# Two list parts scattered under the attention, and counts read into registers as steps of the plan

## The chip, the cores and the metric

The kernel runs on one core of one Trainium2 chip. The metric is device time in microseconds (us); the times before are the median of three runs. The engines are named as the profile names them: PE (TensorE; PEld is its weight load), DVE (VectorE), ACT (ScalarE), POOL (GpSimd) and SP (SyncE, which issues DMAs).

## What is computed

The reference is one transformer block with adaptive layer norms, on 2 x 2048 tokens of 256 features in float32: a causal attention with two query heads that share keys and values, and then a mixture of eight experts (hidden width 1024) in which a token goes to each expert whose gate exceeds a threshold of its own. Cut to what matters:

```python
h = _layernorm(x) * (1 + ca) + sa
x = x + ga * attention(h)                       # 2 heads of 128, causal
h = _layernorm(x) * (1 + cb) + sb
gate = softmax(h @ Wg + bg)                     # 8 experts
thr = sigmoid(h @ Wt + bt) * 0.125              # one threshold for each token
w = (gate - thr) * (gate - thr >= 0)
w = w / sum(w)                                  # where the sum is not 0
y = gelu(einsum('td,edf->etf', h, W1) + b1)
out = einsum('te,etd->td', w, einsum('etf,efd->etd', y, W2) + b2)
x = x + gb * out
```

How many tokens an expert gets is known only when the gates have been computed. The kernel computes each expert on its own tokens alone.

## The kernel before

**Attention, as a plan.** The first part (`attention`) treats 32 tiles of 128 tokens. Each piece of work is a step given to a small planner (`Plan`): its engine, an estimated cost, the steps that it comes after, and a rank. The planner plays the steps through with these costs, lets an engine that is free take the ready step of lowest rank, and the instructions of each engine are then issued in that fixed order. `late` is a time after the end of a step before its followers count as ready. Tiles go in groups of four (the last ones of two and one), alternating between the two batches; the tile number is the rank.

For each tile, POOL computes the two inverse deviations of the layer norms (`rstda`, `rstdf`, L418 and L419) and splits the normed features into halves (`hp`, L677) for storing in `feats`. PE turns the normed tile `hx` (`ph`, L692) for the gates.

**Lists.** Each expert has a list in HBM, of token number and weights. `place` holds where an entry goes in the list of each expert, `entry` what is written. A column of `place` belongs to one tile. List 0 is filled under the attention: after each group, `gate_steps` computes the places (L804) and adds one POOL step for each tile (`scatter`, L807), an indirect DMA of 128 entries, ranked ten behind the group. The first 512 tokens of expert 0 (`AHEAD` items) are worked on at the end of the attention, where that many are there. The last steps compute the counts (`total`, L849 to L868): the tokens of each expert, the number of its whole items less one, capped at eight (`more`), and eight less that.

**Experts, as programs.** The second part (`experts`) is five programs, one for each engine, that loop over items of 256 tokens and wait for one another by semaphores. The number of rounds is read at run time from the tile `counts` into registers (`count`, which calls `values_load`, L1035); PE, ACT and DVE read all the counts of the experts at the beginning of their programs. DVE increments `ready` for the first time only after its nine reads, and PE waits for it before its first matmul.

For an item, POOL copies its indices (`at`, L1296), gathers its 256 rows from `feats` (`xr`, L1254), SP transposes them (`xp`, L1100), DVE joins the halves to `xT` (L1196), PE multiplies with the first weights (`h`, L1142) and the second ones (`y`, L1133), with ACT's gelu between (`g`, L1168), DVE forms the weighted result `yo` (L1232), and POOL adds it to the output with two indirect DMAs (`out`, L1285). `xT`, `xp`, `xr` and `yo` exist once. The weights of expert e + 2 are loaded by ACT when it begins expert e (L1177, L1180). An expert's last item may be a half one, of 128 tokens.

The lists of experts 1 to 7 are written here, each during the expert before, in eight parts of four columns (`write`, L1267 to L1275: two copies and four indirect DMAs). POOL hands out a part in each of an expert's first items; parts for which there are too few items go ahead of them (`front`). Expert 0's program writes the first part of list 1 once more at its very start, before the counts are read:

```python
write(1, 0, 0)
skip = count(pool, 3 * E, AHEAD * CI)
```

SP reads a list into its sheet (`read`, L1090) once all its parts have landed. Between the two parts of the kernel all engines meet (L1075, L1418).

Of the kernel before, what the change touches and what calls it, by code (L numbers as in the profile page):

```python
# [18 lines left out]
ALU = mybir.AluOpType  # L19
# [13 lines left out]
NW = 4  # L33
NP = NTOK // P // NW
AHEAD = 2
AHEAD_TILES = 24
SC = 512
EPS = 1e-5
# [63 lines left out]
def adaln_block_kernel(ctx, tc, x, wqkvT, woT, wgt, bgt, w1, b1T, w2, b2, cT, wmod, rope, out):  # L102
# [49 lines left out]
        yo=[const.tile([P, CI, D], F32, name=f"yo_{k}") for k in range(AHEAD)],  # L152
        who=const.tile([P, CI], I32, name="who"),
        xT=const.tile([P, KD, TI], F32, name="xT"),
    )

    with tc.manual_schedule():
# [35 lines left out]
def attention(  # L193
# [522 lines left out]
    def gate_steps(b, i0, m, q, group, after):  # L716
# [86 lines left out]
            nc.vector.tensor_scalar(col, col, 7, None, ALU.logical_shift_right)  # L803
            nc.vector.tensor_tensor(dst, dst, col, ALU.add)  # L804

        def scatter(j):
            nc.gpsimd.indirect_dma_start(  # L807
                out=lists[0],
                out_offset=bass.IndirectOffsetOnAxis(ap=place[:, at + j, 0:1], axis=0),
                in_=entry[:, at + j, 0, :],  # L810
                in_offset=None,
            )

# [105 lines left out]
    for k in range(AHEAD):  # L919
# [71 lines left out]
        for c in range(CI):  # L991
            for f0 in (0, NF // 2):
# [4 lines left out]
                    give=["s"] * (NF // 2) if (c, f0) == (CI - 1, NF // 2) else [],  # L997
                )
        low("DVE", 1.5, result, [n, n_g, l_b2], give=["ps", "size"])

    n_s = low(
        "SP", 0.1, lambda: nc.sync.dma_start(kept.sheet, sheet_of_0), listed, late=2.0
# [10 lines left out]
            next_at, next_at, flag[:, 0:1], number[:, :CI], ALU.mult, ALU.add  # L1013
        )

    n = low("DVE", 0.4, behind, [n_s, n_flag])
    fetch(lambda c: next_at[:, c : c + 1], "_next", [n], lambda: kept.xT)

    plan.add("PE", 0.2, total, after=[last, n_flag], take=["ps"], give=["ps"], rank=q)
    plan.run()  # L1020
    ctx.close()


def experts(
# [5 lines left out]

    LAG = 2
    xT, who, yo = kept.xT, kept.who, kept.yo[-1]

    def count(eng, at, most):
        return nc.values_load(  # L1035
            counts[0:1, at : at + 1], engines=[eng.engine],
            skip_runtime_bounds_check_because="from a sum of 0s and 1s over all tokens",
            min_val=0, max_val=most,
        )

    def run(eng, many, most, do):
        with eng.If(many > 0):
# [32 lines left out]
    with tc.tile_critical():  # L1075
# [7 lines left out]
        with nc.Block() as block:  # L1083

            @block.sync
            def _(sync):
                def read(e):

                    sync.wait_ge(sem["written"], (e * NP + 1) * (16 * NW))
                    sync.dma_start(  # L1090
                        sheets[e], lists[e].rearrange("(p c) f -> p c f", p=P)
                    ).then_inc(sem["read"], 16)

                def turn(t):

                    sync.wait_ge(sem["loaded"], t * (16 * CI))
                    sync.sem_inc(sem["paused"], 1)
                    sync.wait_ge(sem["ready"], t + 1)
                    sync.sem_inc(sem["paused"], 1)
                    sync.dma_start_transpose(xp, xr).then_inc(sem["planed"], 16)  # L1100

                sync.sem_inc(sem["planed"], 16)
                done, t0 = 1, 0
                for e in range(E):
                    many = items_of(sync, count(sync, e, NTOK))
                    if e == E - 1:
                        run(sync, many, NTOK // TI, lambda i: turn(t0 + i))
                    else:
                        a = count(sync, E + e, NP)
# [12 lines left out]

            @block.tensor
            def _(pe):
# [29 lines left out]
                        pe.wait_ge(here[e], 32)  # L1154

                pe.sem_inc(sem["taken"], 1)
                n = [count(pe, e, NTOK) for e in range(E)]
                items(pe, n, item, begin)

            @block.scalar  # L1160
            def _(act):
# [20 lines left out]
                        ).then_inc(here[e + RES], 16)  # L1182

                act.sem_inc(sem["second"], 4)
                items(act, [count(act, e, NTOK) for e in range(E)], item, begin)

            @block.vector
            def _(dve):
# [48 lines left out]
                    if e > 0:  # L1237
                        dve.wait_ge(sem["read"], 16 * e)

                n = [count(dve, e, NTOK) for e in range(E)]  # L1240
                skip = count(dve, 3 * E, AHEAD * CI)
                dve.sem_inc(sem["ready"], 2)
                items(dve, n, item, begin)

# [1 line left out]
            def _(pool):  # L1246
# [11 lines left out]
                            in_offset=bass.IndirectOffsetOnAxis(ap=at[:, c : c + 1], axis=0),  # L1258
                        ).then_inc(sem["loaded"], 16)

                def write(e, c, w=None):

                    if w is None:
                        w = c + (e - 1) * NP
                        wait("written", w * (16 * NW) + 16 * NW)
                        w = w + 1
                    pool.tensor_copy(  # L1267
                        to, place[:, ds(c * NW, NW), e : e + 1].rearrange("p c o -> p (c o)")
                    ).then_inc(sem["staged"], 1)
# [55 lines left out]
                            compute_op=ALU.add,  # L1325
                        ).then_inc(sem["added"], 16)
                pool.sem_inc(sem["biased"], AHEAD)
                write(1, 0, 0)
                skip = count(pool, 3 * E, AHEAD * CI)
                done, t0 = 1, 0  # L1330
                for e in range(E):
                    many = items_of(pool, count(pool, e, NTOK))
                    if e > 0:
                        wait("read", 16 * e)
                    if e == E - 1:
                        run(pool, many, NTOK // TI, lambda i: item(e, i, t0 + i))
                    else:
                        a, front = count(pool, E + e, NP), count(pool, 2 * E + e, NP)

                        def part(c):  # L1340
                            write(e + 1, nc.s_assert_within(c, 0, NP - 1,
                                skip_runtime_bounds_check_because="a part of a list"))
# [20 lines left out]
                add(t0)  # L1363

                single = pool.snap(
                    ((count(pool, E - 1, NTOK) + (P - 1)) >> 7) & 1, min_val=0, max_val=1
                )
                with pool.If(single > 0):
                    add(t0 + 1, 1)
# [52 lines left out]
```

## Time and profile before

| | us |
|---|---|
| median of three runs (lowest to highest) | 1696.54 (1695.61 to 1699.3) |
| the profiled execution | 1694.8 |
| its span in the profile | 1693.0 |
| attention and the work ahead, until PE's first h of L1142 | 526.1 |
| experts' programs, from there to the end | 1166.9 |

In the profile a row of the timeline has the start, the duration (both in us), the engine, the line of the kernel, the operation, and what it writes and reads; in brackets stands how long the engine was idle before it and what released it. A row of the waits has the engine and line that waited, what it waited for, the sum in us, how often, and the longest. A row of the chain has start, duration and what. A row of the windows has the stretch, its length, the busy time of PE, PEld, DVE, ACT and POOL with the number of instructions, the granted PE clock, the DMA share and GB/s. A name with q (PEldq) is an engine's sequencer: there the three durations are the least, the median and the most, in ns.

### The profile page before, as it was taken

How to read it: one execution, taken by the hardware profiler on the slowest of the kernel's cores; microseconds unless marked ns; L12 is line 12 of the kernel's file. 1: busy time of each engine (PE TensorE's matmuls, PEld its weight loads, DVE VectorE, ACT ScalarE, POOL GpSimd, SP SyncE). 2: the span in 40 equal slices, each digit the busy share in tenths (PEclk: the TensorE clock that was granted, in tenths of full speed). 3: DMA queues.
4: the chain of work that ended last, by engine and by line, in shares of the span. 5: the costliest groups of instructions: out<-in, count | busy, mean ns of one | idle time of the engine just before them, and what ended most of it. 6: DMA issues, size and time to landing. Idle time of an engine off the chain costs nothing.

```text
span 1693.0 us, 26695 instructions
## 1 busy us (share of the span) xinstructions
PE 1627.9 (96%) x7666; PEld 1354.3 (80%) x7666; DVE 677.9 (40%) x2220; ACT 575.1 (34%) x1390; POOL 855.9 (51%) x991
## 2 busy tenths in 40 slices
PE   6898999999998997999999999999999999999997
PEld 3666666677777886888888888888888888888886
DVE  5886666566652322223332222223222232222322
ACT  1544555555551222222222222222322232222222
POOL 2332322111125777765776775676677467744443
PEclk9999999999999998999999999999999999999998
DMA  6310100000013335333434533433533343333333
GB/s 210 102 36 26 38 20 29 22 11 19 14 40 92 59 62 109 56 63 62 103 61 64 109 59 66 106 61 59 106 59 59 65 63 57 64 56 59 65 56 47
DMA packets 166046, 106.36 MB, mean 63 GB/s; under 512 B 111137, under 2 KB 157345, under 8 KB 165857
## 3 DMA queue, kind: packets, MB, share of 16 engines
q0 software_dynamic: 42064, 46.84, 17.3%
q1 hardware_dynamic: 116048, 46.22, 11.8%
q10 hardware_dynamic: 7872, 12.58, 2.3%
q8 instruction: 26, 0.43, 0.1%
q14 instruction: 36, 0.29, 0.1%
HBM read 50.39 MB, written 31.87 MB: 49 GB/s over the span
## 4 chain that ended last, share of the span: by engine, by line
PE 60%; DMA 3%; POOL 2%; issue 2%; POOLq 0%; DVE 0%; SPq 0%; DVEq 0%
PE h L1142 30%; PE y L1133 30%; DMA xp<-xr 2%; POOL out L1285 1%; DMA xr<-feats,at 1%; POOL list L1275 0%; DMA out<-yo,who 0%; POOL xr L1254 0%; POOLq L1035 0%; POOL out L1317 0%; POOL at L1296 0%; POOLq L1083 0%; POOLq L1296 0%; DVE yo L1232 0%; DVE xT L896 0%
## 5 line engine op out<-in xcount | busy, mean ns | idle before, releaser
L1142 PE MATMUL h<-xT,w 128*128 128x256 f32 (+1 forms) x2752 | 659.8, 373 | 16.3 <-DVE xT L1196 9.0
L1133 PE MATMUL y<-w,g 128*128 128x256 f32 x2640 | 654.2, 379 | 0.0
L1168 ACT ACTIVATE g<-h,b_sb 128x256 f32<-128x256 f32 (+1 forms) x688 | 319.6, 465 | 847.5 <-PE h L1142 844.8
L1142 PEld LDWEIGHTS h<-xT,w 128*128 128x128 f32 x2752 | 515.6, 192 | 85.4 <-DVE xT L1196 10.5
L1133 PEld LDWEIGHTS y<-w,g 128*128 128x128 f32 x2640 | 499.2, 190 | 65.2
L1285 POOL DMA_INDIRECT out<-yo,who x173 | 283.0, 1636 | 212.8 <-DVE yo L1232 160.6
L1196 DVE COPY xT<-xp 128x512 uint16<-128x512 uint16 x172 | 68.4, 439 | 613.9 <-PE h L1142 581.2
L1275 POOL DMA_INDIRECT list<-new,to x228 | 235.4, 1032 | 99.3 <-POOL new L1270 46.7
L1254 POOL DMA_INDIRECT xr<-feats,at x172 | 173.7, 1010 | 100.9 <-POOL at L1296 70.2
L611 PE MATMUL pav<-pT,v 128*128 128x256 f32 x544 | 144.8, 389 | 0.5 <-ACT pT L605 0.5
L528 PE MATMUL psc<-kT,qT 128*128 128x512 f32 (+3 forms) x320 | 144.2, 536 | 0.6 <-ACT qT L517 0.2
L539 DVE TENSOR_SCALAR_CACHE_REDUCE s<-psc 128x512 f32<-128x512 f32 (+3 forms) x160 | 95.8, 605 | 78.1 <-PE psc L528 59.2
L555 ACT ACTIVATE s<-s,nmx 128x512 f32<-128x512 f32 (+3 forms) x160 | 103.8, 651 | 53.7 <-DVE nmx L546 53.4
L611 PEld LDWEIGHTS pav<-pT,v 128*128 128x128 f32 x544 | 95.9, 192 | 26.3 <-issue 16.4
L1220 DVE TENSOR_TENSOR yb<-y,b_bc 128x256 f32<-128x256 f32 x165 | 62.7, 420 | 132.4 <-PE y L1133 132.4
L605 ACT COPY pT<-ptr 128x512 f32<-128x512 f32 (+1 forms) x144 | 76.8, 563 | 50.9 <-PE ptr L601 28.9
L418 POOL TENSOR_SCALAR rstdf<-mvf 128x1 f32<-128x1 f32 x32 | 8.7, 270 | 166.7 <-DVE mvf L414 70.5
L807 POOL DMA_INDIRECT list<-entry,place x32 | 33.8, 1056 | 101.3 <-DVE place L804 75.1
L601 PEld LDWEIGHTS ptr<-ident,s 128*128 128x128 f32 x544 | 65.4, 143 | 21.3 <-ACT s L555 8.7
L601 PE MATMUL ptr<-ident,s 128*128 128x128 f32 x544 | 76.6, 277 | 4.5 <-ACT s L555 4.4
L1211 DVE SCALAR_TENSOR_TENSOR gate<-gb_bc,mcur,part 128x256 f32<-128x256 f32 x172 | 75.8, 482 | 3.0
L528 PEld LDWEIGHTS psc<-kT,qT 128*128 128x128 f32 x320 | 56.9, 191 | 15.3 <-issue 6.2
(157 smaller groups left out, 1076.1 us busy)
## 6 DMA issues: line engine op xcount, KB each, us to landing
w<-in_w ACTq DMA_DIRECT2D x12, 1024.0 KB, 8.0
x<-in_x SPq DMA_DIRECT2D x32, 128.0 KB, 2.1
out<-x SPq DMA_DIRECT2D x32, 128.0 KB, 1.7
w<-in_w SPq DMA_DIRECT2D x4, 1024.0 KB, 9.1
feats<-hp SPq DMA_DIRECT2D x32, 128.0 KB, 1.7
list<-new,to POOLq DMA_INDIRECT x228
out<-yo,who POOLq DMA_INDIRECT x173, 3.9
xr<-feats,at POOLq DMA_INDIRECT x172, 2.8
```

The source lines that it names most:

```text
L528: nc.tensor.matmul(ps[:, :w], st["qT"][:, h, :], kT[:, ds(c * SC, w)], start=True, stop=not last)
L539: nc.vector.tensor_scalar(s[:, :w], st["sc", h, c][:, :w], 1.0, None, ALU.mult, ALU.max, accum_out=st["mx", h][:, c : c + 1],)
L555: nc.scalar.activation(s[:, :w], s[:, :w], AF.Exp, bias=st["nmx", h], accum_out=st["den"][:, h, c : c + 1],)
L601: nc.tensor.transpose(ptr[:, j, h, :], s[:, ds((c0 + j) * P % SC, P)], ident)
L605: nc.scalar.copy(pT[:, :m], st["ptr", c0][:, :m])
L611: nc.tensor.matmul(st["pav"][:, : NH * P], v[:, c0 + j, :], st["pT", c0][:, j].rearrange("p h t -> p (h t)"), start=(c0 + j == 0), stop=(c ...
L1133: last = pe.matmul(ys[c], gs[f % 4][:, ts(c, P)], weights[e][1][:, f, :], start=(f == 0), stop=(f == NF - 1),)
L1142: last = pe.matmul(hs[f % 4][:, :w], weights[e][0][:, k, ts(f, P)], xT[:, k, :w], start=(k == 0), stop=(k == KD - 1),)
L1168: act.activation(gs[f % 4][:, :w], hs[f % 4][:, :w], AF.Gelu_apprx_tanh, bias=b1_sb[:, at : at + 1],).then_inc(sem["act"], 1)
L1254: pool.indirect_dma_start(out=xr[:, ts(c, 2 * D)], out_offset=None, in_=feats, in_offset=bass.IndirectOffsetOnAxis(ap=at[:, c : c + 1], ax ...
L1275: pool.indirect_dma_start(out=lists[e], out_offset=bass.IndirectOffsetOnAxis(ap=to[:, j : j + 1], axis=0), in_=new[:, j, :], in_offset=Non ...
L1285: pool.indirect_dma_start(out=rows, out_offset=bass.IndirectOffsetOnAxis(ap=who[:, c : c + 1], axis=0), in_=yo[:, c, :], in_offset=None, b ...
```

## The change

It has two parts.

Parts 0 and 1 of list 1 (columns 0 to 7, the first eight tiles of batch 0) are scattered under the attention, as eight POOL steps ranked twenty behind their groups, of which there are two (the first and the third). In the experts' programs the writing of list 1 starts with part 2; part 0 is no longer written twice. The counts of expert 0 are cut accordingly: at most five parts go with items.

The register reads of the counts become the last steps of the plan (`hold`), one for each engine, ranked behind all else; `count` then takes the register that is held. PE's step comes after the last matmul of the work ahead, ACT's after its last gelu there, DVE's after `behind`, POOL's after `total`, SP's after its read of list 0's sheet. POOL and SP hold those of expert 0 alone.

```diff
+FRONT = 2
...
-        def scatter(j):
+        def scatter(e, j):
             nc.gpsimd.indirect_dma_start(
-                out=lists[0],
-                out_offset=bass.IndirectOffsetOnAxis(ap=place[:, at + j, 0:1], axis=0),
-                in_=entry[:, at + j, 0, :],
+                out=lists[e],
+                out_offset=bass.IndirectOffsetOnAxis(ap=place[:, at + j, e : e + 1], axis=0),
+                in_=entry[:, at + j, e, :],
...
             listed.append(plan.add(
-                "POOL", 1.27, lambda j=j: scatter(j), after=[n], rank=r + 10.0, late=3.0
+                "POOL", 1.27, lambda j=j: scatter(0, j), after=[n], rank=r + 10.0, late=3.0
             ))
+        for j in range(m):
+            if at + j < FRONT * NW:
+                plan.add(
+                    "POOL", 1.27, lambda j=j: scatter(1, j), after=[n], rank=r + 20.0, late=3.0
+                )
...
+        nc.vector.tensor_scalar(n[:, :1], n[:, :1], float(NP - 1 - FRONT), None, ALU.min)
         nc.vector.tensor_copy(counts[:, E : 2 * E], n)
         nc.vector.tensor_scalar(
-            counts[:, 2 * E : 3 * E], n, -1.0, float(NP), ALU.mult, ALU.add
+            counts[:, 2 * E : 2 * E + 1], n[:, :1], -1.0, float(NP - 1 - FRONT), ALU.mult, ALU.add
+        )
+        nc.vector.tensor_scalar(
+            counts[:, 2 * E + 1 : 3 * E], n[:, 1:], -1.0, float(NP), ALU.mult, ALU.add
         )
...
+    def hold(name, eng, columns):
+        def load():
+            kept.count[name] = {at: register(nc, eng, counts, at) for at in columns}
+
+        return load
+
+    skip = 3 * E
+    low("PE", 2.0, hold("PE", nc.tensor, range(E)), [n_total] + n_ahead)
+    low("ACT", 2.0, hold("ACT", nc.scalar, range(E)), [n_total] + n_a)
+    low("DVE", 2.2, hold("DVE", nc.vector, [*range(E), skip]), [n_total, n_behind])
+    low("POOL", 1.0, hold("POOL", nc.gpsimd, [skip, 0, E, 2 * E]), [n_total])
+    low("SP", 0.5, hold("SP", nc.sync, [0, E]), [n_total, n_s])
     plan.run()
...
-                    sync.wait_ge(sem["written"], (e * NP + 1) * (16 * NW))
+                    sync.wait_ge(sem["written"], (e * NP - FRONT) * (16 * NW))
...
-                def write(e, c, w=None):
-
-                    if w is None:
-                        w = c + (e - 1) * NP
-                        wait("written", w * (16 * NW) + 16 * NW)
-                        w = w + 1
+                def write(e, d):
+
+                    first = FRONT if e == 1 else 0
+                    w = d + ((e - 1) * NP - FRONT if e > 1 else 0)
+                    c = d + first if isinstance(d, int) else nc.s_assert_within(
+                        d + first, first, NP - 1,
+                        skip_runtime_bounds_check_because="a part of a list",
+                    )
+                    if e > 1 or not isinstance(d, int):
+                        wait("written", w * (16 * NW))
...
-                write(1, 0, 0)
-                skip = count(pool, 3 * E, AHEAD * CI)
+                write(1, 0)
+                skip = count(pool, 3 * E)
...
-                        run(pool, front, NP, part)
+                        most = NP - 1 - FRONT if e == 0 else NP
+
+                        def part(d):
+                            d = nc.s_assert_within(d, 0, most - 1,
+                                skip_runtime_bounds_check_because="a part of a list")
+                            write(e + 1, d + 1 if e == 0 else d)
+
+                        run(pool, front, most, part)
```

More of the change, by code (lines that the diff above doesn't have):

```diff
@@ L154, in adaln_block_kernel @@
         xT=const.tile([P, KD, TI], F32, name="xT"),
+        count={},
     )
@@ L999, in attention @@
         low("DVE", 1.5, result, [n, n_g, l_b2], give=["ps", "size"])
+        n_ahead = [n]
     n_s = low(
@@ L1014, in behind, with register @@
         )
-    n = low("DVE", 0.4, behind, [n_s, n_flag])
-    fetch(lambda c: next_at[:, c : c + 1], "_next", [n], lambda: kept.xT)
-    plan.add("PE", 0.2, total, after=[last, n_flag], take=["ps"], give=["ps"], rank=q)
+    n_behind = low("DVE", 0.4, behind, [n_s, n_flag])
+    fetch(lambda c: next_at[:, c : c + 1], "_next", [n_behind], lambda: kept.xT)
+    n_total = plan.add(
+        "PE", 0.2, total, after=[last, n_flag], take=["ps"], give=["ps"], rank=q, late=2.0
+    )
[9 more added lines that the diff above has]
+    low("SP", 0.5, hold("SP", nc.sync, [0, E]), [n_total, n_s])
     plan.run()
     ctx.close()
+def register(nc, eng, counts, at):
+    return nc.values_load(
+        counts[0:1, at : at + 1], engines=[eng.engine],
+        skip_runtime_bounds_check_because="from a sum of 0s and 1s over all tokens",
+        min_val=0, max_val=NTOK if at < E else NP if at < 3 * E else AHEAD * CI,
+    )
 def experts(
@@ L1032, in experts, with count @@
     xT, who, yo = kept.xT, kept.who, kept.yo[-1]
[L1034 to L1039, printed above, removed]
+    eng_name = {
+        nc.tensor.engine: "PE", nc.scalar.engine: "ACT", nc.vector.engine: "DVE",
+        nc.gpsimd.engine: "POOL", nc.sync.engine: "SP",
+    }
+    def count(eng, at):
+        held = kept.count[eng_name[eng.engine]]
+        return held[at] if at in held else register(nc, eng, counts, at)
     def run(eng, many, most, do):
@@ L1104, in _ @@
                 for e in range(E):
-                    many = items_of(sync, count(sync, e, NTOK))
+                    many = items_of(sync, count(sync, e))
                     if e == E - 1:
@@ L1108, in _ @@
                     else:
-                        a = count(sync, E + e, NP)
+                        a = count(sync, E + e)
                         run(sync, a, NP, lambda i: turn(t0 + done + i))
@@ L1156, in _ @@
                 pe.sem_inc(sem["taken"], 1)
-                n = [count(pe, e, NTOK) for e in range(E)]
+                n = [count(pe, e) for e in range(E)]
                 items(pe, n, item, begin)
@@ L1184, in _ @@
                 act.sem_inc(sem["second"], 4)
-                items(act, [count(act, e, NTOK) for e in range(E)], item, begin)
+                items(act, [count(act, e) for e in range(E)], item, begin)
             @block.vector
@@ L1238, in begin @@
                         dve.wait_ge(sem["read"], 16 * e)
-                n = [count(dve, e, NTOK) for e in range(E)]
-                skip = count(dve, 3 * E, AHEAD * CI)
+                n = [count(dve, e) for e in range(E)]
+                skip = count(dve, 3 * E)
                 dve.sem_inc(sem["ready"], 2)
@@ L1259, in gather @@
                         ).then_inc(sem["loaded"], 16)
-                def write(e, c, w=None):
-                    if w is None:
-                        w = c + (e - 1) * NP
-                        wait("written", w * (16 * NW) + 16 * NW)
-                        w = w + 1
+                def write(e, d):
[4 more added lines that the diff above has]
+                        skip_runtime_bounds_check_because="a part of a list",
+                    )
+                    if e > 1 or not isinstance(d, int):
+                        wait("written", w * (16 * NW))
                     pool.tensor_copy(
@@ L1327, in _ @@
                 pool.sem_inc(sem["biased"], AHEAD)
-                write(1, 0, 0)
-                skip = count(pool, 3 * E, AHEAD * CI)
+                write(1, 0)
+                skip = count(pool, 3 * E)
                 done, t0 = 1, 0
                 for e in range(E):
-                    many = items_of(pool, count(pool, e, NTOK))
+                    many = items_of(pool, count(pool, e))
                     if e > 0:
@@ L1337, in _ @@
                     else:
[L1338 to L1342, printed above, removed]
-                        run(pool, front, NP, part)
+                        a, front = count(pool, E + e), count(pool, 2 * E + e)
+                        most = NP - 1 - FRONT if e == 0 else NP
[4 more added lines that the diff above has]
+                        run(pool, front, most, part)
                         run(pool, a, NP, lambda i: item(
@@ L1365, in _ @@
                 single = pool.snap(
-                    ((count(pool, E - 1, NTOK) + (P - 1)) >> 7) & 1, min_val=0, max_val=1
+                    ((count(pool, E - 1) + (P - 1)) >> 7) & 1, min_val=0, max_val=1
                 )
```

## The prediction

> **What bounds the kernel now.** I read the page's busy shares first, then TensorE's waits from 480 to 660 us, then the timeline there.
>
> ```profile
> PE 1627.9 (96%) x7666; PEld 1354.3 (80%) x7666; DVE 677.9 (40%) x2220; ACT 575.1 (34%) x1390; POOL 855.9 (51%) x991
> ```
> ```profile
> PE h L1142 <- DVE xT L1196: 9.0, 1, 9.0
> PE h L1142 <- DVEq L1035: 7.3, 1, 7.3
> ```
>
> TensorE (PE) is the bound. In the experts' programs it waits twice: 7.3 us at their start, on the loads of L1035, and 9.0 us for xT at the change from expert 0 to 1. After 660 us no PE wait is listed. A gain must come from these two; a loss can also come from the attention.
>
> ```profile
> 526.11 4.70 PE L1142 MATMUL h<-xT,w 128*128 128x256 f32 x12 [7.34 <-DVEq L1035]
> 541.88 2.75 PE L1142 MATMUL h<-xT,w 128*128 128x256 f32 x12
> ...
> 654.74 5.24 PE L1142 MATMUL h<-xT,w 128*128 128x256 f32 x12 [8.99 <-DVE xT L1196]
> ```
> ```profile
> 540.71 0.76 DVE L1196 COPY xT<-xp 128x512 uint16<-128x512 uint16 x2 [12.41 <-DMA xp<-xr]
> ```
>
> Item 1 starts at 541.88, and its xT is complete only at 541.47: behind the first wait stands a second chain, with 0.4 us of slack. After a wait, twelve h matmuls take 4.5 to 5.1 us (to the next y) against 2.6 otherwise: each wait also costs a cold clock.
>
> ```profile
> 605.42 3.08 DMA xp<-xr
> ...
> 643.52 2.75 DMA xr<-feats,at
> 646.50 7.34 DMA xp<-xr
> ```
> ```profile
> 599.55 0.77 POOL L1296 COPY at<-sheet 128x2 int32 x1
> ...
> 603.48 0.20 POOL L1267 COPY to<-place 128x4 int32 x1
> ...
> 613.16 0.77 POOL L1296 COPY at<-sheet 128x2 int32 x1
> ```
>
> The chain of waits and POOL's timeline say why xT is late at 654. An item of expert 0 with its list part takes POOL 613.16 - 599.55 = 13.6 us, hardly less than PE's 13.81 (555.69 - 541.88). Expert 0's last item is a half one (7 us of PE), so POOL is late there; the gather comes at 643.5 and its transpose meets the weight load that ScalarE issued at 644.50: 7.3 us instead of 3.1.
>
> **The boundary: -11.6 us.** Expert 0 has 9 items, so all 8 parts of list 1 now go into items 1 to 8, after a first part that is written twice. With FRONT = 2 one goes ahead and five into items 1 to 5; items 6 to 8 carry none: 12 scatters and 6 copies fewer on POOL (four of the scatters were the double part's, eight are moved). A part takes POOL from 603.48 to about 609.9, 6.4 us. Items 1 to 5 run as before. In item 6 POOL is through with the gather by 603.5 and meets add(6), which waits for item 4's yo, before at 602.7 to 603.4; from there POOL, freed of 3 x 6.4 us, waits for VectorE's yo and no longer the other way. The yo of item 6 comes at about 626.5 (y ends at 624.7, then yb 0.8, yo 0.7). The two out scatters take 3.6 us, three counts of expert 1 that are still loaded in place about 1 us: POOL reads item 9's indices at 631.5 instead of 641.16. Gather and landing end at 637, when xp comes free (xT of item 8 is copied at 636.27 to 637.04), and the transpose at 640.5, before the weights start. xT then waits for the half item's h, as at the later boundaries. SyncE's read of list 1 moves from behind turn 8 to behind turn 5 (about 592) and waits there for the last part's landing (about 597); turn 6, queued behind it, is due at 605. PE's y ends at 645.6, item 9 runs 13.81 warm, item 10 starts at 659.4; it started at 671.04. The 11.6 are 9.1 of wait and 2.5 of cold clock. Next due is item 10's transpose, beside the weights: issued at 650.5, at worst 7.3 us, 0.8 of copy, so 658.6 against 659.4.
>
> **The loads: -0.3 us, and +2.0 of clock.**
>
> ```profile
> L1035 DVEq TENSOR_LOAD <-counts x9: 301/311/631, 522.2 to 525.5; - x9
> L1035 PEldq TENSOR_LOAD <-counts x8: 301/306/568, 522.1 to 524.9; - x8
> ```
> ```profile
> L1418 PEldq EVENT_SEMAPHORE x12: 51/51/4409, 514.7 to 1692.9; - x12
> ```
>
> VectorE's nine loads (3.6 us) hold back `ready`, and so PE. As plan steps they hide: VectorE stands idle from 512.0 to 518.81, ScalarE from 512.7, POOL from 505.2 to 512.23, SyncE between 506.9 and 516.4. Queued behind them are VectorE's result and xT copy, POOL's gather and SyncE's transpose, all due later. PE's eight (3.1 us) stand behind its last matmul in order, which ends at 518.77; but its queue reached the entry barrier at 514.7, so it runs 4 us ahead and is done by 518. The entry stays at 521.1, set by VectorE's xT copy. Were the cover gone, VectorE's loads behind `result` would move the entry by 3.6 us, PE's behind the matmuls by up to 0.9. I take 0. Two more small VectorE operations in `total` (0.16 us each at 508) lie under PE's matmuls, which run to 518.77: nothing.
>
> PE can then start at about 522.4 instead of 526.11. But POOL's road to item 1's xT (two out scatters, part, gather, transpose) starts at the entry and has no such load in it: POOL's own run beside its scatters. xT stays at 541.47, item 1 starts at about 541.6: 3.7 us earlier at the start becomes 0.3 at item 1.
>
> Instead PE idles twice: 518.77 to 522.4 (3.6 us), and before item 1 3.4 us (after a cold item 0) or 5.4 (after a warm one). Rows for the clock, PEclk being the third figure from the end:
>
> ```profile
> 518.80:526.10 7.30, 0.00 (x0) 0.00 (x0) 2.19 (x6) 0.00 (x0) 3.15 (x4) 0.79 0.23 26
> ...
> 128.40:132.70 4.30, 0.00 (x0) 0.02 (x1) 0.62 (x3) 0.04 (x1) 1.85 (x4) 0.75 0.11 31
> ...
> 174.30:176.50 2.20, 0.01 (x1) 0.04 (x1) 0.61 (x3) 0.82 (x2) 1.59 (x4) 1.00 0.20 55
> ```
>
> If full is 1.0 and cold 0.5, the clock fell 4.2, 2.1 and, in 2.2 us, not at all after the work ended. [...] Item 0's cold clock costs nothing, as xT hides it; item 1's costs 2.0 (526.11 to 541.88 is 15.77 against 13.81). Ends 0 and 2.5; I take 2.0, nearest to the 4.3 us row.
>
> **Eight scatters in the attention: +2.5 us.**
>
> ```profile
> 130.16 0.96 POOL L807 DMA_INDIRECT list<-entry,place  x1 [2.08 <-DMA list<-entry,place]
> 131.14 0.25 POOL L418 TENSOR_SCALAR rstdf<-mvf 128x1 f32<-128x1 f32 x1
> ```
> ```profile
> 132.71 0.66 PE L692 MATMUL ph<-ident,hx 128*128 128x128 f32 x2 [4.39 <-DVE nmx L546]
> ```
>
> A scatter waits for the landing of its predecessor in the same list: the pitch is 2.4 us (222.04, 224.41), where the planner counts 1.27. The eight take place and entry where they lie, without the copies of L1267 and L1270. Four go behind the scatters at 80 to 89 us, four behind those at 169 to 177, 19 us of POOL in all. Behind them stand rstda, rstdf and hp; PE waits in order for hx, which needs rstdf. Before, 24 scatters of list 0 were followed by five PE waits at such an rstdf: 1.3, 4.4, 2.2, 1.6 and 1.9, 11.4 us, and two cold restarts of 2: 0.64 each, so 5 for eight. The new ones rank 10 behind these and can use gaps of 2 to 6 us at 93 to 104 and 178 to 200, where one rstdf each loses about a scatter's landing (1.4). Ends: -1 (the planner's order changes, for the better by chance) and 8; I take 2.5.
>
> **Sum.** -11.6 - 0.3 + 2.0 + 2.5 = -7.4. The profiled execution took 1694.8 (span 1693.0), so 1687.4; the median of the runs is 1696.54, 1.7 above it, so 1689.1 there. Ends: -12.9 and, with everything dear, -1.4.
>
> **Rivals.**
> - *Scatters stop PE.* Each of the eight costs PE its whole pitch: 19.2 us at 80 to 105 and 169 to 200. Then -11.6 + 1.7 + 19.2 = +9.3: 1706. It turns slower once more than 9.9 us reach PE. For it: five such waits exist. Against: of the 24 scatters' 58 us of pitch, 15 reached PE, cold clock included, and those met more rstdf than the new ones will.
> - *The boundary stall stays in part.* If POOL gains only about 5 of its 9.7 us, the transpose still meets the weights: 4.5 us of wait and the cold clock stay, -11.6 + 7.0 + 4.2 = -0.4: 1696. Against it: three items without a part.
> - *No second chain.* If POOL's loads did delay its chain, item 1 also starts 3.7 earlier and warm: -11.6 - 3.7 + 2.5 = -12.8: 1683.7. Against it: scatters at 1.3 us pitch from 527.34 to 531.23, as elsewhere.
> - *The loads do not hide.* Entry 3.6 later: about 1692.7; part of the forecast's upper end.
>
> **How the numbers follow.** Forecast 0.70, scatters 0.10, stall in part 0.11, no second chain 0.09. A measurement here can tell about 0.2% (3.4 us) from no change. Faster: 0.70 + 0.09 + 0.01 = 0.80; same: 0.09 of the partial stall + 0.03 = 0.12; slower: 0.08. Range 1684 to 1695: the forecast's ends, leaving out most of the scatters' case.
>
> **What would show it.** Right: no PE wait near 640, twelve h in 2.6 us there; 216 scatters at the list write; PE's first h near 522.4, then a wait of 3 to 5 us before item 1. Wrong: item 1 starting well before 541; new PE waits at ph near 90 to 105 and 180 to 200; an entry after 522.

## The result, and the profile after

The changed kernel takes 1688.1 us, median of six runs (1685.82 to 1691.1), against 1696.09 (1695.61 to 1699.3) for the kernel before in six runs beside it: a ratio of 0.9951, 95% interval 0.9938 to 0.9964, so about 8 us less. The forecast was 1689.1. The profiled execution took 1689.65 us with a span of 1687.8, which is 5.2 below the span before; the stages below are made from the two profiles and explain these 5.2. The other 2.8 us between the medians are the spread of single executions: the profiled one lies 1.55 above its median, the one before 1.3 below the median of its six. That the median came within 1.0 us of the forecast is therefore in part luck: by the profiles the gain is 2.2 us smaller than the 7.4 forecast.

Below, items are counted from PE's first h on (item 0, 1, 2 and so on), and the boundary is the change from expert 0 to expert 1. The busy shares, then PE's waits from 480 us to the end:

```profile
PE 1633.7 (97%) x7666; PEld 1355.8 (80%) x7666; DVE 678.1 (40%) x2222; ACT 575.6 (34%) x1390; POOL 848.9 (50%) x981
```
```profile
PE h L1180 <- DVEq L1280: 4.7, 1, 4.7
PE h L1180 <- DVE xT L1234: 2.4, 1, 2.4
```

Of the two waits of before, 7.3 and 9.0, the first is 4.7 now and the second is gone. The 2.4 us are a new one, at another place. PE's timeline shows where (h is L1180 now, the last y of the attention L975):

```profile
515.60 7.07 PE L975 MATMUL pya<-w,s_g 128*128 128x256 f32 x32
...
527.41 5.29 PE L1180 MATMUL h<-xT,w 128*128 128x256 f32 x12 [4.74 <-DVEq L1280]
546.30 4.39 PE L1180 MATMUL h<-xT,w 128*128 128x256 f32 x12 [2.37 <-DVE xT L1234]
...
651.66 2.75 PE L1180 MATMUL h<-xT,w 128*128 128x256 f32 x12
665.47 2.75 PE L1180 MATMUL h<-xT,w 128*128 128x256 f32 x12
```

The wait of 2.37 stands before item 1, as forecast. At the boundary (651.66, 644.63 + 7.03 after the half item's start) PE goes on without a gap and warm (twelve h in 2.75 us; the clock granted from 651.6 to 654.4 us was 1.00). Why, VectorE's and POOL's timelines say:

```profile
545.44 0.80 DVE L1234 COPY xT<-xp 128x512 uint16<-128x512 uint16 x2 [16.45 <-DMA xp<-xr]
...
650.66 0.76 DVE L1234 COPY xT<-xp 128x512 uint16<-128x512 uint16 x2 [2.35 <-PE h L1180]
```
```profile
633.59 1.81 POOL L1327 DMA_INDIRECT out<-yo,who  x1 [6.74 <-DVE yo L1270]
...
636.74 0.76 POOL L1338 COPY at<-sheet 128x2 int32 x1
```

The copy of xT at the boundary now waits for the half item's h, no longer for a transpose, and POOL stands 6.74 us idle ahead of it, waiting for VectorE's yo.

The stages, all in us. The last column is the span's end less item 10's start.

| | last y of the attention ends | from there to item 2 | item 2 to item 10 | item 10 to the end |
|---|---|---|---|---|
| before | 518.77 | 36.92 | 115.35 | 1021.96 |
| after | 522.67 | 39.08 | 103.72 | 1022.33 |
| difference | +3.90 | +2.16 | -11.63 | +0.37 |
| forecast | +2.5 | +1.7 | -11.6 | 0 |

The sum is -5.2, where the forecast had -7.4.

In the attention, two of the new scatters stand ahead of an rstdf, and PE waits behind (POOL's timeline, then PE's):

```profile
96.57 0.97 POOL L809 DMA_INDIRECT list<-entry,place  x1 [1.40 <-DMA list<-entry,place]
97.56 0.25 POOL L420 TENSOR_SCALAR rstdf<-mvf 128x1 f32<-128x1 f32 x1
...
178.00 0.96 POOL L809 DMA_INDIRECT list<-entry,place  x1 [1.43 <-DMA list<-entry,place]
178.99 0.24 POOL L420 TENSOR_SCALAR rstdf<-mvf 128x1 f32<-128x1 f32 x1
```
```profile
99.12 0.41 PE L694 MATMUL ph<-ident,hx 128*128 128x128 f32 x2 [1.19 <-DVE nmx L548]
...
180.46 0.44 PE L694 MATMUL ph<-ident,hx 128*128 128x128 f32 x2 [2.71 <-DVE nmx L548]
```

Each of these two scatters stands still for 1.4 us until the one before it in the same list has landed. The two waits of PE are new, but they are not where the 3.9 us went: summed over the attention, PE idles less than before. The windows from the start to the last y (before, then after):

```profile
0.00:518.77 518.77, 482.29 (x2274) 342.85 (x2274) 336.12 (x1268) 255.49 (x702) 116.58 (x217) 0.98 0.15 47
```
```profile
0.00:522.67 522.67, 488.29 (x2274) 346.65 (x2274) 336.79 (x1270) 255.82 (x702) 125.27 (x225) 0.97 0.15 47
```

Length less PE's busy time is its idle time: 36.5 us before, 34.4 after. In the other order of the steps some old waits are shorter (4.39 us at 132.71 before, 1.54 at 129.79 after). The busy time of the same 2274 matmuls, however, is 6.0 us longer, at a lower granted clock (0.97 in the second row, 0.98 in the first). The stretch from 180 to 245 us shows most of it (before, then after):

```profile
180.00:245.00 65.00, 63.06 (x308) 44.39 (x306) 46.56 (x172) 34.52 (x98) 15.96 (x31) 1.00 0.10 31
```
```profile
180.00:245.00 65.00, 60.35 (x261) 41.23 (x262) 38.71 (x144) 31.40 (x87) 15.24 (x26) 0.89 0.07 21
```

There the granted clock was 0.89 instead of 1.00; an estimate from these two rows is 0.11 of 65 us, about 7 us. PE waits 2.71, 1.91 and 2.19 us for a ph in it. That these waits brought the clock down is not shown: e8 below has 1.58, 1.91 and 2.19 us there, and 0.97.

The loads now run under the attention (by line; the three durations are the least, the median and the most in ns, then from when to when the loads began):

```profile
L1054 PEldq TENSOR_LOAD <-counts x8: 299/308/615, 518.6 to 521.8; - x8
L1054 DVEq TENSOR_LOAD <-counts x9: 301/306/555, 515.6 to 518.9; - x9
```

PE's are done at 522.1, 0.5 us before its last matmul ends (522.67): hidden, but only just.

### The profile page after: what moved, and what is told of

Read it like the earlier page. It is cut to its first block, busy times and chain, and to the rows that moved or that the text cites. A ratio compares the mean times of both kernels' runs of the same rounds, so it can differ in the third digit from the quotient of the medians.

```text
span 1687.8 us, 26670 instructions
## 1 busy us (share of the span) xinstructions
PE 1633.7 (97%) x7666; PEld 1355.8 (80%) x7666; DVE 678.1 (40%) x2222; ACT 575.6 (34%) x1390; POOL 848.9 (50%) x981
## 4 chain that ended last, share of the span: by engine, by line
PE 66%; DMA 1%; issue 1%; POOL 0%; POOLq 0%; DVE 0%; DVEq 0%; SPq 0%
PE h L1180 33%; PE y L1171 33%; DMA out<-yo,who 0%; DMA xp<-xr 0%; POOL list L1317 0%; DMA xr<-feats,at 0%; POOL out L1359 0%; POOLq L1121 0%; DVE yo L1270 0%; POOL out L1327 0%; DVE xT L1234 0%; DVE yb L1258 0%; POOLq L1463 0%; POOL xr L1292 0%; DVEq L1121 0%
## 5 line engine op out<-in xcount | busy, mean ns | idle before, releaser
L1180 PE MATMUL h<-xT,w 128*128 128x256 f32 (+1 forms) x2752 | 659.3, 372 | 7.1 <-DVEq L1280 4.7
L1180 PEld LDWEIGHTS h<-xT,w 128*128 128x128 f32 x2752 | 514.0, 191 | 77.3 <-DVEq L1280 5.1
L1317 POOL DMA_INDIRECT list<-new,to x216 | 219.5, 1016 | 94.0 <-POOL new L1312 44.2
L809 POOL DMA_INDIRECT list<-entry,place x40 | 41.5, 1038 | 109.9 <-DVE place L806 72.1
```

The lines of the kernel that those rows point to most:

```text
L1180: last = pe.matmul(hs[f % 4][:, :w], weights[e][0][:, k, ts(f, P)], xT[:, k, :w], start=(k == 0), stop=(k == KD - 1),)
L1317: pool.indirect_dma_start(out=lists[e], out_offset=bass.IndirectOffsetOnAxis(ap=to[:, j : j + 1], axis=0), in_=new[:, j, :], in_offset=Non ...
```

## The experiments

They ran on three chips, on each of which the kernel before is slower than in the runs of the result: 1714.04 (58 runs), 1720.3 (49) and 1719.3 us (19). The first four kernels shared one chip, the next four a second, the last four a third. PE has additional waits there, of up to 2.8 us (e6, at 643.51) and most of them inside half items, so the columns behind item 2 are read for the boundary's wait, and not to the microsecond. The columns ahead of item 2 are nearly free of them. One table for all (ratios against before on the same chip; an interval that leaves out 1 tells a gain from none, and overlapping intervals do not rank two kernels):

| kernel | last y ends | to item 2 | item 2 to 10 | item 10 to end | median, ratio [95%] |
|---|---|---|---|---|---|
| e1: parts alone | 521.81 | 37.37 | 107.32 | 1040.7 | 1706.44, 0.9951 [0.9936, 0.9965] |
| e2: loads alone | 518.53 | 37.59 | 118.30 | 1035.8 | 1712.09, 0.9984 [0.9968, 0.9999] |
| e3: FRONT = 0 | 518.68 | 39.27 | 107.30 | 1046.2 | 1706.79, 0.9958 [0.9944, 0.9972] |
| e4: FRONT = 4 | 524.12 | 39.13 | 107.28 | 1035.1 | 1706.4, 0.9953 [0.9931, 0.9975] |
| the change again | 523.08 | 39.10 | 110.30 | 1040.9 | 1710.08, 0.994 [0.9919, 0.996] |
| e5: first part once, no more | 519.48 | 37.07 | 110.93 | 1040.3 | 1713.36, 0.9954 [0.9936, 0.9971] |
| e6: gather first | 521.58 | 34.11 | 112.32 | 1035.6 | 1706.62, 0.9918 [0.9887, 0.9948] |
| e7: gather first, FRONT = 0 | 518.11 | 33.86 | 106.38 | 1054.8 | 1710.61, 0.9947 [0.9929, 0.9965] |
| e8: scatters to lists of their own | 518.34 | 37.55 | 108.98 | 1040.0 | 1706.67, one run |
| before again | 519.51 | 37.23 | 118.40 | 1049.5 | 1726.41, one run |
| e9: gather first, FRONT = 1 | 525.39 | 38.45 | 110.44 | 1042.0 | 1717.88, 0.9989 [0.9971, 1.0006] |
| e6 again | 520.12 | 34.11 | 108.47 | 1037.5 | 1704.12, 0.9909 [0.9886, 0.9933] |

The theory: the boundary gives 11.6 because POOL has less to write there; the loads give next to nothing, since POOL's road to item 1's xT stands behind them; the scatters cost what PE waits for behind their landings. The rivals: the loads bring part of the gain; the eight scatters are what frees the boundary; the attention's cost is the issue of the scatters or the planner's other order.

**e1, the parts alone.** The change, with the register reads left in the programs.

```diff
-    low("PE", 2.0, hold("PE", nc.tensor, range(E)), [n_total] + n_ahead)
...
-    low("SP", 0.5, hold("SP", nc.sync, [0, E]), [n_total, n_s])
```

> The list parts moved and the double part dropped, the counts loaded in the programs as before. Theory (the gain is the boundary alone): PE's wait of 9.0 us for xT at the change of experts is gone, with its cold clock (-11.6); the attention ends 3.9 later, at 522.7; the wait of 7.3 at the start stays: 1696.1 - 7.7 = 1688.4, no slower than with the loads moved. Rival (the loads moved bring half of the gain): 1692 or more.

No wait for xT at the boundary nor before item 1, 37.37 to item 2 (36.92 before), and the whole gain against the kernel before: the edits of the lists carry it. Which of these edits does, e3 and e5 ask.

**e2, the loads alone.** The kernel before, with `hold` and the five steps, and list 1 written as before.

> Only the counts' loads moved into the plan; lists written as before. Theory (behind the loads stands POOL's road to item 1's xT): PE's first matmul comes 2 to 3 us sooner, but item 1 starts no earlier, some 0.5 us later, and runs cold (+1.6); the 9.0 at the change of experts stays: about +2, 1698. Rival (the loads were the bound): item 1 starts 2 to 3.7 us earlier, 1692 to 1694.

PE's timeline of e2:

```profile
523.20 4.54 PE L1171 MATMUL h<-xT,w 128*128 128x256 f32 x12 [4.67 <-DVEq L1271]
542.20 2.86 PE L1171 MATMUL h<-xT,w 128*128 128x256 f32 x12 [3.24 <-DVE xT L1225]
...
657.88 5.48 PE L1171 MATMUL h<-xT,w 128*128 128x256 f32 x12 [10.90 <-DVE xT L1225]
```

PE starts 2.7 us sooner behind the last y (4.67 of wait against 7.34) and gives it back before item 1; item 2 comes 0.7 later than before. The boundary's wait stays. The loads alone bring nothing by the stages ahead of item 2; the ratio's interval holds a gain of up to 0.3%, which these stages do not show.

**e3, FRONT = 0.** No scatters in the attention; the first part is still written once.

```diff
-FRONT = 2
+FRONT = 0
```

> FRONT = 0: no list-1 scatter in the attention; the first part, written once, ahead of item 1 and seven parts in items 1 to 7; loads moved. Theory (one part less, 6.4 us of POOL, is enough to bring the transpose before the weights): attention ends at 518.8 again, no wait at the change of experts, start as with the change (+2.1): 1696.1 - 11.6 + 2.1 = 1686.6, and faster than the change by the attention's 3.9 less what reordering does. Rival (three items without a part are needed): 4 us or more of the wait stay, 1691 or more.

The attention ends where it ended before (518.68), and the boundary has no wait for xT:

```profile
641.15 1.50 PE L1180 MATMUL h<-xT,w 128*128 128x128 f32 x12
...
651.34 2.85 PE L1180 MATMUL h<-xT,w 128*128 128x256 f32 x12
```

So the scatters under the attention are not what frees the boundary. Writing the first part once instead of twice leaves one part of eight off the items; that is enough. It was expected to be faster than the change by what the attention no longer loses. The whole run does not show that (0.9958, against 0.9951 in e1): its last stretch is 1046.2.

**e4, FRONT = 4.**

```diff
-FRONT = 2
+FRONT = 4
```

> FRONT = 4: sixteen list-1 scatters in the attention instead of eight, three parts left in items. Theory (each scatter holds POOL by its predecessor's landing and costs PE about 0.5 us): attention ends near 526.6 (+7.8 against before), nothing more to gain at the change of experts: 1688.1 + 3.9 = 1692. Rival (the 3.9 are a chance effect of the planner's new order, not of the scatters): the attention's end moves by less than 2 us or back, 1686 to 1690.

524.12 instead of the 526.6 expected: twice the scatters cost less than twice, as far as one profile tells. PE idles 34.3 us in the attention, no more than with eight. Nothing more is gained at the boundary.

**The change again**, beside the next three.

> The changed kernel once more, beside the others on this chip: ratio to before 0.995, attention's last y ends near 522.7, item 1 waits 2.4 us for xT and begins cold.

It gives 0.994 [0.9919, 0.996] on this chip, with the stages ahead of item 2 within 0.4 us of the first profile (523.08 and 39.10).

**e5, the first part once and nothing else.** FRONT = 0, and the register reads in the programs.

> FRONT = 0 and the loads in the programs as before: all that is left of the change is that the first part of list 1 is written once. Theory (the boundary is the whole gain, the scatters and the moved loads each take some back): last y ends at 518.7, wait of 7.3 at the start, item 1 without a wait and warm, no wait for xT at the change of experts: -11.6, ratio 0.993, 2 to 6 us faster than the change. Rival (the parts of the change help each other): no faster than the change, 0.995 or more.

A wait for xT is not there at the boundary (653.66, no bracket), the attention ends at 519.48 and the start takes 37.07: this one edit gives 0.9954 [0.9936, 0.9971], and the two parts that the change is named for add nothing that can be told from it. By the stages e5 is 5.0 us ahead of the change at item 10 (667.48 against 672.48), as expected; as a whole the expected 2 to 6 us are not there, and its median is 3.3 us above the change's, with intervals that overlap.

**e6, the gather first.** In the change, POOL writes a part of list 1 ahead of item 1's gather. Here it goes behind it (two lines that cut the counts to match are left out).

```diff
-                write(1, 0)
...
+                        if e == 0:
+                            item(0, 1, 1, lambda: write(1, 0))
+                            run(pool, pool.snap(a - 1, min_val=0, max_val=NP - 1), NP - 1,
+                                lambda i: item(0, i + 2, i + 2, lambda: part(front + i)))
```

> The change, with one difference: list 1's first part of the programs is no longer written ahead of item 1's gather but behind it (it counts on expert 0 having an item 1, as it has here). Theory (POOL's road to item 1's xT makes the moved loads worthless): xT of item 1 comes about 6 us earlier, before item 0 ends; item 1 starts about 20.5 us after the last y instead of 23.6 and warm, so 3.1 + 1.6 = 4.7 us faster than the change, ratio 0.992. Rival (something else holds item 1, such as the entry or the first weights): item 1 waits as before, 0.995.

Item 1's gather is issued 2.6 us behind the start of the last out scatter, instead of 8.6 (529.15 to 537.76 after), and PE goes from item 0 to item 1 without a wait and warm, its twelve h in 2.75 us (POOL's timeline, VectorE's, PE's):

```profile
528.06 1.58 POOL L1359 DMA_INDIRECT out<-yo,front  x1 [0.30 <-issue]
529.11 0.73 POOL L1338 COPY at<-sheet 128x2 int32 x1
530.69 1.03 POOL L1292 DMA_INDIRECT xr<-feats,at  x1 [0.85 <-POOL at L1338]
532.03 0.99 POOL L1292 DMA_INDIRECT xr<-feats,at  x1 [0.30 <-issue]
```
```profile
539.58 1.03 DVE L1234 COPY xT<-xp 128x512 uint16<-128x512 uint16 x2 [11.68 <-DMA xp<-xr]
```
```profile
526.27 4.54 PE L1180 MATMUL h<-xT,w 128*128 128x256 f32 x12 [4.70 <-DVEq L1280]
541.87 2.75 PE L1180 MATMUL h<-xT,w 128*128 128x256 f32 x12
```

34.11 instead of 39.10: the second chain was the part on POOL's road. With it out of the way item 2 comes 2.8 us sooner behind the last y than in the kernel before, and 5.0 sooner than in the change. The gather first with the reads still in the programs was not run; there, as e1 and e5 show, PE has no wait before item 1 that it could take away. This kernel has the lowest ratios of the study, 0.9918 [0.9887, 0.9948] here and 0.9909 [0.9886, 0.9933] on the third chip; the intervals overlap with the change's 0.9919 to 0.996.

**e7, the same with FRONT = 0.**

> As the run before, with FRONT = 0: no list-1 scatter in the attention, all eight parts in items 1 to 8. Theory: attention's 3.9 us come back and the start keeps its gain, but item 8 carries a part again, so POOL may be late at the change of experts: with no wait there 8 us faster than the change, 0.990; with half of the wait left 0.993. Rival (the parts ahead matter for more than the boundary): a wait of 5 us or more for xT near 645.

The best start (518.11, then 33.86), but POOL is a little late again at the boundary, with one part more in the items: 1.71 us of wait for xT, warm (the twelve h behind it take 2.86 us). By the stages ahead of item 10 it is the fastest of its four (658.35 against 668.01 for e6); the run as a whole is not, and 0.9947 misses the expected 0.990 to 0.993. It takes 1054.8 us from there on, for which this study has no explanation but the scattered waits.

**e8, scatters to lists of their own.** The eight scatters stay in the plan with their cost and rank, but each writes a scratch list of its own, which nothing reads, and list 1 is written by the experts' programs alone. The order of the attention's instructions is that of the change on every engine.

```diff
-                out=lists[e],
+                out=kept_.scratch[at + j] if e else lists[0],
...
-            if at + j < FRONT * NW:
+            if at + j < 8:
```

> The change with FRONT = 0 (no part of list 1 is written in the attention, all of them in the experts' programs), but the eight scatter steps stay in the attention's plan with the same cost, ranks and followers; each writes its tile's entries of expert 1 into a scratch list of its own, which nothing reads. So POOL's order is the change's, and none of the eight waits for the landing of a predecessor in its list. Theory (the cost of the scatters is the 1.4 us for which a scatter stands still until the one before it in its list has landed, and what waits behind it): the attention's last y ends near 519.5 to 520.3, eight times about 0.2 us of issue at most above the 518.5 to 518.7 without scatters. Rival (it is the planner's other order, or the issue of 1 us each): it ends at 521.6 to 523.1, as with the change. Half-way (521) would mean both. At the boundary from expert 0 to 1 no wait for xT, as with FRONT = 0 before (107.3 us from item 2 to item 10).

518.34, below the 519.5 to 520.3 expected, below all five runs of that order in which the eight share a list (520.12 to 523.08) and level with no scatters. POOL's timeline and PE's:

```profile
177.00 0.95 POOL L811 DMA_INDIRECT scratch<-entry,place  x1 [0.30 <-issue]
178.25 0.96 POOL L811 DMA_INDIRECT scratch<-entry,place  x1 [0.30 <-issue]
179.24 0.24 POOL L422 TENSOR_SCALAR rstdf<-mvf 128x1 f32<-128x1 f32 x1
```
```profile
180.71 0.44 PE L696 MATMUL ph<-ident,hx 128*128 128x128 f32 x2 [1.58 <-DVE nmx L550]
```

The pitch is 1.25 where the change has 2.4, the wait of 2.71 is 1.58, and that at 99 us is gone. PE's window up to the last y:

```profile
0.00:518.34 518.34, 486.83 (x2274) 346.94 (x2274) 336.67 (x1270) 256.23 (x702) 125.71 (x225) 0.98 0.15 47
```

PE idles 31.5 us here, against 34.4 to 36.6 in the five runs (mean 35.3): the waits for landings cost this order 3.8 us of PE's time. The issue of the scatters and the order cost nothing in sum, but the order is not neutral. Against the six kernels without new scatters (mean idle time 35.4, mean busy time 483.5) it saves 3.9 us of idle time and costs 3.3 of busy time. That e8 comes out level is those two cancelling, in one run; the five runs of the same order differ by 3 us among themselves.

**Before again**, on the third chip.

> The kernel before once more, on the chip of these runs. If the scattered waits of PE inside half items, which the runs of the experiments show after 660 us and the first two profiles do not, belong to the chip, this run has them too, and takes 1035 us and more from item 10 to the end (1022.0 in the first profile) with 36.9 us from the last y of the attention to item 2 and 115.4 from there to item 10. If they belong to the edits, it takes 1022 for the last stretch.

It has the scattered waits too (PE's waits from 660 us on; the first profile of this kernel lists none there):

```profile
PE y L1133 <- ACT g L1168: 11.9, 11, 2.4
PE y L1133 <- issue: 4.8, 3, 2.1
```

So they come without the edits, with the chip or the occasion; what causes them is open. Ahead of item 2 the stages are those of the first profile (519.51 and 37.23).

**e9, gather first with FRONT = 1**, to see whether half the scatters cost half.

```diff
-FRONT = 2
+FRONT = 1
```

> FRONT = 1 (four scatters in the attention instead of eight), register reads in the plan, and the part of list 1 that POOL writes ahead of the items put behind item 1's gather. Theory: last y of the attention near 520.3 (half-way between the 518.5 of no scatters and the 522.7 of eight), 34 us from there to item 2 (start warm and without a wait at item 1), no wait for xT at the boundary from expert 0 to 1, so 2 us less than the same kernel with FRONT = 2 and about 8 less than the kernel before, by stages; as a whole 0.991 to 0.994 of before. Rival (the order of the attention jumps with the number of scatters rather than growing): last y outside 519.3 to 521.3.

The theory missed and the rival holds: four scatters end the attention at 525.39, later than eight or sixteen, and here PE's idle time is what grew (40.7 us). The planner, which counts 1.27 us for each scatter, arrives at another order on PE, and in it a group's four scatters of list 0 stand together ahead of an rstdf that PE needs (POOL's timeline, then PE's):

```profile
220.10 0.96 POOL L809 DMA_INDIRECT list<-entry,place  x1 [1.43 <-DMA list<-entry,place]
222.48 0.96 POOL L809 DMA_INDIRECT list<-entry,place  x1 [1.41 <-DMA list<-entry,place]
225.46 0.96 POOL L809 DMA_INDIRECT list<-entry,place  x1 [2.02 <-DMA list<-entry,place]
226.44 0.25 POOL L420 TENSOR_SCALAR rstdf<-mvf 128x1 f32<-128x1 f32 x1
```
```profile
228.01 0.46 PE L694 MATMUL ph<-ident,hx 128*128 128x128 f32 x2 [4.40 <-DVE hx L672]
```

The last gates come late too: the sum of the counts (L856) is at 516.48 against 507.76 in e6 again. So the gather for item 0 is late, its xT copy starts at 529.75, 4.4 us behind the last y instead of 1.5, and the first h waits 7.56 instead of 4.69. Nothing is left of the gain: 0.9989 [0.9971, 1.0006].

**e6 again**, beside e9.

> The change with the ahead part of list 1 behind item 1's gather (as in the earlier run of it), beside the version with FRONT = 1 on the same chip. By stages: last y at 521.6, 34.1 to item 2, 112 to item 10 where the chip has waits of its own there, 104 where it has none. If four scatters in the attention cost half of eight, this is 1 to 2 us slower than FRONT = 1; if the order decides, the difference can have either sign. Against before 0.990 to 0.994.

0.9909 [0.9886, 0.9933]; from the last y to item 2 it takes 34.11 once more.

## Why the prediction was right, and where its terms were off

**The boundary, -11.6: right to the tenth, and by its own steps.** Item 2 starts 6.06 us later after than before (561.75 against 555.69). With that taken off, POOL reads item 9's indices at 630.7 (forecast 631.5), item 9 starts at 645.6 (645.6) and item 10 at 659.4 (659.4). POOL waits for VectorE's yo, and xT for the half item's h, as said. What the forecast did not say, and e3 and e5 show: one part less is enough, so the scatters in the attention were not needed for it. Its working put three items without a part into the sum without asking how many of them it takes.

**The loads, -0.3 at item 1: +0.5 came.** The mechanism was right: the reads are hidden, the second chain stands, PE waits before item 1, and e6 shows it by taking the chain away. Two terms were small misses. The entry (the last engine's arrival at the meeting) stands 2.26 us behind the last y in both kernels, as forecast. But POOL's first out scatter starts 3.04 behind the start of the xT copy of L907, where it was 2.38:

```profile
522.65 1.64 POOL L1317 DMA_INDIRECT out<-yo,front  x1 [8.18 <-issue]
```
```profile
527.21 1.64 POOL L1359 DMA_INDIRECT out<-yo,front  x1 [8.85 <-issue]
```

(Before, then after; the xT copies start at 520.27 and 524.17.) All kernels with the reads in the plan have 3.03 or 3.04, all with them in the programs 2.37 or 2.38, e1 and e5 among them. In the two traces the meeting of the engines has more semaphore steps with the reads in the plan (nine of POOL's in the chain instead of five, 0.08 to 0.09 us apart). The forecast had called the entry unchanged and costed these steps at nothing. PE is later out of the meeting as well: its branch stands 3.6 us behind the last y (L1463 at 526.3), where it stood 2.9 behind (L1418 at 521.7). That is 0.7 of the 1.1 us by which PE's first h, 4.74 behind the last y, misses the forecast's 3.6. The rest is a reading of the forecast: before, VectorE's reads ended at 525.8, but PE's own register steps (L1043) still ran at 526.0. So PE's own eight reads, 3.4 us, were last, and not VectorE's nine. In sum PE waits 2.37 before item 1 and not 3.4: 1.1 for the later start, 0.8 for an item 0 that took 16.5 us instead of 15.8, and 0.8 the other way because xT is later.

**The cold clock at item 1, +2.0: +1.6 came.** Item 1 takes 15.45 instead of 13.81. The windows of after (stretch, length, busy PE, PEld, DVE, ACT, POOL, granted clock, DMA share, GB/s):

```profile
543.90:546.30 2.40, 0.03 (x2) 0.01 (x1) 0.86 (x3) 0.00 (x0) 1.81 (x2) 0.94 0.34 59
546.30:550.60 4.30, 4.30 (x13) 3.55 (x14) 0.60 (x2) 0.95 (x2) 3.37 (x3) 0.63 0.40 36
```

A gap of 2.4 us, shorter than the 3.4 forecast, was followed by a lower clock here, 0.63. (The two levels that the forecast set are in the trace of before: 1.00 granted from 521.0 to 523.0 us, 0.50 from 524.0 to 526.1.) A gap of 3.2 us at the same place in e2 was followed by 1.00:

```profile
538.90:542.20 3.30, 0.06 (x2) 0.00 (x1) 0.86 (x3) 0.00 (x0) 2.41 (x3) 1.00 0.43 81
542.20:545.20 3.00, 3.00 (x14) 2.66 (x15) 0.60 (x2) 1.05 (x3) 2.67 (x3) 1.00 0.31 33
```

The forecast's 2.0 was an estimate between its ends of 0 and 2.5. The size came out near, but a gap of 2.4 us came before a clock of 0.63 and one of 3.2 before 1.00, so the length of the gap did not tell which of the two was due. That part was luck.

**The scatters, +2.5: +3.9 came**, within its ends of -1 and 8. The five profiles of this order end at 521.85 on the mean, the six profiles without new scatters at 518.85: 3.0, so the size was good. The mechanism was right only in part. A scatter ahead of an rstdf does wait 1.4 us for a landing (1.40 and 1.43 in after), PE does wait behind it, and e8 shows that without the landings PE idles 3.8 us less in this order. But the forecast added these waits to those of before, and the new order took as much away elsewhere: PE's idle time is 35.3 us on the mean of the five and 35.4 on that of the six. The 3.0 us are all in the busy time of its matmuls (486.6 against 483.5 on the means), with the granted clock lower: from 60 to 490 us, in six stretches weighed by their length, it was 0.974 on the mean of the five and 0.984 on that of four of the six (before, e2, e3, e5). The forecast had the clock only as a part of its 0.64 for each scatter. That the sum met its size is luck as much as working. That it would grow with the number was tacit in the forecast, and e9 shows that it does not have to.

**Its signs of being wrong.** Two of those that it named did show. New PE waits at ph came at 99 and 180 us, 1.2 and 2.7 long. The forecast had itself put a cost on such waits, so they do not contradict its sum. The entry came after 522 (at 524.9), only because the attention ended 3.9 us later. Of the signs of being right, the wait before item 1 was 2.4 us and not 3 to 5; PE without a wait near 640 and the 216 scatters at the list write came as said.

**The rivals.** Scatters that stop PE for their whole pitch (19 us) did not happen, with sixteen neither. The boundary's stall did not stay in part. That there is no second chain is refuted by e6 and e2. The loads hide.

The sum, then: 11.6 won at the boundary; 3.9 given back in the attention (PE's matmuls 6.0 longer at a granted clock of 0.97 against 0.98, its idle time 2.1 shorter), 2.2 at the start (0.5 of barrier and chain, 1.6 of cold clock), and 0.4 in the rest, which has no wait on PE in either profile and was not traced further.

## What to carry to other kernels

When a wait ends last, look for the second one close behind it before counting a gain: here a chain with 0.4 us of slack stood behind 3.6 us of loads. Moving the loads alone gained nothing, and moving one list part behind one gather then gained 5 us. Ask how little of an edit does the work: one part written once instead of twice freed the boundary, and the eight scatters were a cost. An added step in a planned schedule has two costs, its own and that of the new order; the second had either sign here (in e8 3.9 us less idle time of PE and 3.3 more busy time) and was known only from the trace of that very order. Sum an engine's idle and busy time over a stage before a loss is put down to single waits: here the waits only changed places, and the time was lost at a lower granted clock (0.97 against 0.98).

## What was not expected of the hardware

- A PE gap of 2.4 us was followed by a clock of 0.63 (after) and one of 2.1 us by 0.64 (e3, at 540 us), one of 3.2 us by 1.00 (e2 and e8). In these runs the length of the gap alone did not decide it; what else did was not measured.
- In the attention, indirect scatters into one list stood 2.4 us apart, with 1.4 us of waiting for a landing in between (before, 222.04 and 224.41), and two into lists of their own 1.25 (e8, at 177.00 and 178.25). Those of the experts' programs go into one list too and stood 1.3 apart, with no wait for a landing (before, 527.34 to 531.23).
- Five profiles with the same instructions in the same order in the attention end it between 520.12 and 523.08. The first to end has the longest idle time of PE (36.6 us, against 34.4 to 35.5 in the others). What goes with the end is PE's busy time, 483.5 us in the first and 488.1 and 488.3 in the last two, and the granted clock, 0.98 there and 0.97 here.
- The same kernel before takes 1696.1, 1714.0, 1719.3 and 1720.3 us (medians) in four sets of runs, the last three on three chips; in profiles of these three sets PE has waits of up to 2.8 us, most of them inside half items. In these runs, then, a change of 5 us was readable by stages and only just as a whole.
